# Expert weight loads predicated on the expert of three blocks earlier, in a two-layer graph network with mixtures of experts

## The chip, the cores and the metric

The kernel runs on one core of a Trainium2 chip. The metric is the device time of one execution in microseconds (us), which for one core is the time of that core. A core has TensorE (matrix products, here with a separate record for loading its stationary operand), VectorE, ScalarE, GpSimd and SyncE, each with its own instruction queue that is worked in order, and 16 DMA engines that move data between the device's memory and the on-chip buffer. In the profile they are PE and PEld, DVE, ACT, POOL and SP; "SPq" is SyncE's queue, from which nearly all of this kernel's plain transfers are issued.

## The reference

There are 2708 nodes with 256 features and an adjacency matrix of 2708 x 2708. Two layers follow each other; each has a graph attention and a mixture of experts, both with a residual:

```
x = x + gnn0(layernorm(x), adj)
x = x + moe0(layernorm(x))     # 8 experts, 256 -> 1024 -> 256, gelu, the best 2 of 8 by gate
x = x + gnn1(layernorm(x), adj)
x = x + moe1(layernorm(x))     # 16 experts, 256 -> 512 -> 256, relu, the best 2 of 16
```

The second attention works in hyperbolic coordinates and ends in a sigmoid between exponential and logarithmic maps; the second mixture adds its input and ends in a layer norm with gamma and beta. A mixture computes, for each token, the gate logits, takes the two best experts, and sums their outputs with the softmax of the two logits as weights. All is float32.

## The kernel before

Tokens lie in 22 tiles of up to 128. Each attention multiplies, for a pair of tiles or a tile, the masked weights with all nodes' rows, and accumulates in PSUM. While that runs, the tokens of finished tiles are normalised, gated and routed.

Routing (class `Router`) sorts tokens into pages of 128 rows in device memory, `rows_d`. Tokens are numbered group by group: in layer 0 a group is a pair of tiles, in layer 1 the groups end at tiles 6, 12, 18 and 22. In each group, every expert first fills what is left of its open page and then takes new pages, in the order of the experts. GpSimd scatters each token's row to its two places (L668).

`Experts.plan` gives the pages to blocks: a first stage in page order for pages that are already full (two early stages in layer 1), and the rest when all groups are numbered. It leaves two small tables in the on-chip buffer: `where[0][b]`, the expert of block b, and `where[1][b]`, its first row. Layer 0 works through 47 blocks and layer 1 through 45; a few further blocks (`rest`) stand under a branch that is taken only when more pages are in use.

For a block, `fetch` (L752, L754) brings the 128 rows, `turn` transposes them on TensorE, `hide` (L869) multiplies with the first weights w1, `bend` (L873) applies gelu or relu on ScalarE, `sum_hidden` (L884, L887) multiplies with the second weights w2, `scaled` (L893) weighs on VectorE, and `add` (L898) adds the rows to the sums in device memory by an indirect DMA from GpSimd. Adds of even and odd blocks go to two different sums, and each waits for the last one to the same sums.

The weights of block b go to room b % 3, one of three buffers. `choose` (L734) reads the block's expert from the table into a register of SyncE; `load_w1` (L738) and `load_w2` (L742) issue a DMA each, 1 MB each in layer 0 and 0.5 MB each in layer 1, with the expert as the address's offset. A load of w1 waits until the hidden matmuls of block b - 3 are done, and a load of w2 until its output matmuls are done, since they free the room. Every block loads its weights, whatever is in the room.

The order of each queue is written out while the program is built. In layer 0, `run` sets it by hand: `choose` and w1 of block b + 2, hidden matmuls of b, transposes of b + 1, outputs of b - 1, w2 of b + 2, rows of b + 3. In layer 1, `stream` starts three pieces (`fetcher`, `loader`, `compute`), and a planner (`Clock`) merges them with the routing of the last groups by assumed times. In the steady part of layer 1, SyncE's queue repeats: w2, a row fetch, `choose` of the next block, its w1, its w2. Engines and queues were given a fixed order then (`manual_schedule`), so a wait at the head of SyncE's queue holds all that stands behind it.

After layer 1's blocks the sums are fetched, added on TensorE, normalised, scaled and stored.

Of the kernel before, what the change touches and what calls it, by code (L numbers as in the profile page):

```python
# [13 lines left out]
ET = mybir.EngineType  # L14
# [8 lines left out]
P = 128  # L23
# [123 lines left out]
def kernel(  # L147
# [25 lines left out]
    nc = tc.nc  # L173
# [526 lines left out]
    where = [sm.tile([1, NB_MAX], I32, name=f"where{k}") for k in range(2)]  # L700
# [6 lines left out]
    class Experts:  # L707
# [23 lines left out]
                             w2[:, :n].rearrange("p (c d) -> p c d", d=D))  # L731

        def choose(self, b):
            self.e = nc.values_load(where[0][0:1, b:b + 1], engines=[ET.SP], min_val=0,  # L734
                                    max_val=self.router.E - 1)

        def load_w1(self, b):
            nc.sync.dma_start(self.rooms[b % 3][0], self.w1[bass.ds(self.e, 1)].rearrange(  # L738
                "o (c p) f -> p (o c) f", p=P))

        def load_w2(self, b):
            nc.sync.dma_start(self.rooms[b % 3][1], self.w2[bass.ds(self.e, 1)].rearrange(  # L742
                "o (c p) d -> p (o c) d", p=P))

        def load(self, b):
            self.choose(b)
# [1214 lines left out]
```

## Time and profile before

| | |
|---|---|
| time, median of 3 runs | 1172.25 us (1169.29 to 1180.15) |
| the profiled execution's own time | 1174.49 us |
| its span | 1172.8 us |
| TensorE matmul / weight load busy | 1056.3 us (90%) / 932.1 us (79%) |
| ScalarE / VectorE / GpSimd busy | 586.8 / 528.2 / 404.4 us |
| DMA moved | 261.99 MB, mean 223 GB/s |
| weight loads, layer 0 | 94 of 1024 KB |
| weight loads, layer 1 | 90 of 512 KB |

The page gives each engine's busy time and then cuts the span into 40 slices of 29.3 us, with a digit for the busy share in tenths. A windows answer gives the same for chosen stretches, in us from the start of the span, with the number of instructions in brackets, the granted clock of TensorE, the mean share of the DMA engines in use and their rate. A timeline answer lists instructions in order of time: start, duration, engine, line, operation, output and inputs, and in square brackets the engine's idle time before it with what ended it. A waits answer gives, for an engine and a line, whom it waited for: us in total, times, longest. An answer on one line lists its instructions with the shortest, median and longest duration in ns.

### The profile page before, as it was taken

The page shows a single profiled execution, that of the slowest core. Times are in us where ns is not written, and L with a number is a line of the kernel's source. Part 1 is how long each engine was busy: PE and PEld are TensorE (multiplying, and loading weights), DVE is VectorE, ACT ScalarE, POOL GpSimd, SP SyncE. Part 2 cuts the span into 40 slices and gives each one's busy share as a digit, 9 for nine tenths or more (in the row PEclk, how much of TensorE's full clock was granted, in tenths as well). Part 3 has the DMA queues.
Part 4 walks back from the last instruction along what each step waited for, and adds up shares of the span by engine and source line. Part 5 has one row for each costly group of instructions (what it writes and reads, how often), then busy time and mean ns, then how long its engine had stood idle before and what let it go on. Part 6 is the DMA issues. An engine that isn't in the chain of part 4 may idle for free. (4 is left out here: it accounts for less than half of the span.)

```text
span 1172.8 us, 20834 instructions
## 1 busy us (share of the span) xinstructions
PE 1056.3 (90%) x6753; PEld 932.1 (79%) x6753; DVE 528.2 (45%) x2024; ACT 586.8 (50%) x1637; POOL 404.4 (34%) x467
## 2 busy tenths in 40 slices
PE   5999999988999999999999769998985899999963
PEld 3888888866789999998999634998985788888852
DVE  7778888856531111101111074647677651111136
ACT  3876676644434444444444257536654444444413
POOL 7521121111242222222222250253465375474425
PEclk9999999998999999999999979999897799999987
DMA  9964544410889999999999589401124699999963
GB/s 292 300 226 146 174 146 170 137 77 31 294 268 304 330 321 320 321 287 334 320 323 319 138 274 267 137 1 30 53 82 154 199 266 309 309 311 328 329 194 113
DMA packets 180793, 261.99 MB, mean 223 GB/s; under 512 B 11087, under 2 KB 148982, under 8 KB 177970
## 3 DMA queue, kind: packets, MB, share of 16 engines
q1 hardware_dynamic: 161862, 237.16, 60.9%
q0 software_dynamic: 18816, 23.42, 10.0%
q8 instruction: 57, 0.93, 0.3%
q14 instruction: 58, 0.48, 0.1%
HBM read 205.54 MB, written 54.99 MB: 222 GB/s over the span
## 5 line engine op out<-in xcount | busy, mean ns | idle before, releaser
L893 DVE TENSOR_SCALAR yo<-out_ps,w 128x256 f32<-128x256 f32 x92 | 44.5, 484 | 426.3 <-PE out_ps L887 426.0
L1214 PE MATMUL att_ps<-g_all,z 128*128 128x257 f32 (+3 forms) x968 | 227.6, 388 | 0.0
L1214 PEld LDWEIGHTS att_ps<-g_all,z 128*128 128x128 f32 (+3 forms) x968 | 177.6, 189 | 36.3 <-issue 8.7
L887 PE MATMUL out_ps<-room,ht 128*128 128x256 f32 x872 | 201.6, 383 | 0.0
L887 PEld LDWEIGHTS out_ps<-room,ht 128*128 128x128 f32 x872 | 162.9, 193 | 21.5
L869 PEld LDWEIGHTS hid_ps<-xt,room 128*128 128x128 f32 x1504 | 174.8, 192 | 3.5 <-ACT xt L854 0.8
L869 PE MATMUL hid_ps<-xt,room 128*128 128x128 f32 x1504 | 176.0, 275 | 0.7 <-ACT xt L854 0.5
L1200 ACT ACTIVATE zr<-e_bc,minus_one,g_all 128x256 f32<-128x256 f32 (+3 forms) x242 | 130.7, 591 | 56.8 <-DVE z L1203 56.0
L898 POOL DMA_INDIRECT sums<-yo,xg x43 | 66.9, 1556 | 244.2 <-DVE side L861 131.7
L873 ACT ACTIVATE ht<-hid_ps,w_t 128x128 f32<-128x128 f32 x376 | 128.2, 364 | 23.4 <-PE hid_ps L869 4.1
L668 POOL DMA_INDIRECT rows_d<-xr,place x88 | 92.0, 1046 | 124.7 <-DVE xr L437 77.0
L1565 PE MATMUL att_ps<-half,wide_mask 128*128 128x258 f32 (+1 forms) x968 | 125.9, 292 | 2.4 <-ACT h_all L1502 1.5
L1565 PEld LDWEIGHTS att_ps<-half,wide_mask 128*128 128x128 f32 (+1 forms) x968 | 122.6, 196 | 3.8 <-ACT h_all L1502 2.4
L1203 DVE SCALAR_TENSOR_TENSOR z<-zr,mask_t 128x256 f32<-128x256 f32 (+3 forms) x242 | 98.9, 430 | 32.7 <-ACT zr L1200 17.0
L873 ACT ACTIVATE ht<-hid_ps,w1x 128x128 f32<-128x128 f32 x180 | 65.2, 364 | 96.2 <-PE hid_ps L869 91.6
L898 POOL DMA_INDIRECT sums<-yo,xr x45 | 70.1, 1557 | 82.4 <-DMA sums<-yo,xr 27.8
L863 ACT ACTIVATE w<-xg,side 128x1 f32<-128x1 f32 x43 | 12.7, 295 | 167.6 <-DVE side L861 167.6
L455 PE MATMUL tr_ps<-ident,xr 128*128 128x128 f32 (+1 forms) x222 | 41.1, 296 | 35.0 <-DVE xr L437 15.9
L1425 POOL CAST wide_mask<-mask_t 128x1408 fp32r<-128x1408 fp8e4 x31 | 42.5, 1377 | 84.6 <-PE att_ps L1565 84.6
L869 PE MATMUL hid_ps<-lo,wide_mask 128*128 128x128 f32 x480 | 64.4, 289 | 5.7 <-DMA wide_mask<-in_L_ffn_w_dram 5.5
L869 PEld LDWEIGHTS hid_ps<-lo,wide_mask 128*128 128x128 f32 x480 | 60.5, 202 | 11.2 <-issue 10.5
L455 PEld LDWEIGHTS tr_ps<-ident,xr 128*128 128x128 f32 (+1 forms) x222 | 29.7, 155 | 42.9 <-issue 18.7
(287 smaller groups left out, 1435.6 us busy)
## 6 DMA issues: line engine op xcount, KB each, us to landing
room<-in_L_ffn_W_dram SPq DMA_DIRECT2D x94, 1024.0 KB
wide_mask<-in_L_ffn_w_dram SPq DMA_DIRECT2D x60, 512.0 KB
room<-in_adj_dram SPq DMA_DIRECT2D x20, 1354.0 KB
room<-in_L_ffn_w_dram SPq DMA_DIRECT2D x30, 512.0 KB
rows_d<-nobody SPq DMA_DIRECT2D x1, 7511.0 KB
rows_d<-nobody SPq DMA_DIRECT2D x5, 1295.0 KB
sums<-nobody SPq DMA_DIRECT2D x2, 2944.0 KB
xr<-rows_d SPq DMA_DIRECT2D x45, 129.5 KB
```

Of the source, the lines that this page charges most:

```text
L455: nc.tensor.transpose(ps[:, c, :r], src[:, c * P:(c + 1) * P], ident[:r, :r])
L668: ins = nc.gpsimd.indirect_dma_start(out=self.rows_d[:, :], in_=self.rows[t][:r], in_offset=None, out_offset=bass.IndirectOffsetOnAxis(ap= ...
L869: nc.tensor.matmul(ps[:, :P], w1_b[:, c, f * P:(f + 1) * P], xt[:, c, :], start=(c == 0), stop=(c == DC - 1))
L873: nc.scalar.activation(ht[:, f, :], ps[:, :P], self.func, bias=self.bias[:, f, b:b + 1])
L887: nc.tensor.matmul(ps[:, :D], ht[:, f, :], self.rooms[b % 3][1][:, f, :], start=False, stop=(f == self.FC - 1))
L893: nc.vector.tensor_scalar(yo, ps[:, :D], w, None, op0=OP.mult)
L898: ins = nc.gpsimd.indirect_dma_start(out=self.sums[k][:, :], in_=yo, in_offset=None, out_offset=bass.IndirectOffsetOnAxis(ap=self.rows.pop ...
L1200: nc.scalar.activation(zr[:k, :n], e_bc[:k, lo:lo + n], AF.Relu, bias=minus_one[:k], scale=g_all[:k, j, D + 1:D + 2])
L1203: nc.vector.scalar_tensor_tensor(z[:k, :n], zr[:k, :n], 1.0, mask_t[:k, j // 2, lo:lo + n, j % 2], op0=OP.add, op1=OP.mult)
L1214: nc.tensor.matmul(accs[i][:r, :D + 1], z[:k, q * P:q * P + r], g_all[:k, j, :D + 1], start=(j == 0), stop=(j == LAST))
L1425: nc.gpsimd.tensor_copy(m, src)
L1565: nc.tensor.matmul(accs[i][:, :D + 2], wide_masks[i, j % 2][:k, j // 2, :], half_k[:k, j, :], start=(j == 0 and half_k is halves[0]), stop ...
```

## The change

From block 3 on, `choose` reads a second table entry, the expert of block b - 3, which is the last block that used the same room. Both weight loads of the block get the condition that the two experts differ. Under a false condition the load is to be left out: the address is made to lie outside the weights, and the transfer is to be dropped while its completion is still counted, so that those who wait for it go on. The first three blocks of a layer load as before. No order in any queue is changed and nothing is given to another engine. In the built program, SyncE has per block from 3 on a second register load with its range check, and before each of the two weight loads two register operations more and a fused register operation with four steps where there were two.

```
         def choose(self, b):
-            self.e = nc.values_load(where[0][0:1, b:b + 1], engines=[ET.SP], min_val=0,
-                                    max_val=self.router.E - 1)
+
+            def expert(b):
+                return nc.values_load(where[0][0:1, b:b + 1], engines=[ET.SP], min_val=0,
+                                      max_val=self.router.E - 1)
+
+            self.e = expert(b)
+            self.when = {"cond": self.e != expert(b - 3)} if b >= 3 else {}
 
         def load_w1(self, b):
             nc.sync.dma_start(self.rooms[b % 3][0], self.w1[bass.ds(self.e, 1)].rearrange(
-                "o (c p) f -> p (o c) f", p=P))
+                "o (c p) f -> p (o c) f", p=P), **self.when)
 
         def load_w2(self, b):
             nc.sync.dma_start(self.rooms[b % 3][1], self.w2[bass.ds(self.e, 1)].rearrange(
-                "o (c p) d -> p (o c) d", p=P))
+                "o (c p) d -> p (o c) d", p=P), **self.when)
```

## The prediction

> **What bounds the kernel now.** I read the page's slices first, to find the stages, then the windows, to see what is full in each.
>
> ```profile
> PE   5999999988999999999999769998985899999963
> DMA  9964544410889999999999589401124699999963
> GB/s 292 300 226 146 174 146 170 137 77 31 294 268 304 330 321 320 321 287 334 320 323 319 138 274 267 137 1 30 53 82 154 199 266 309 309 311 328 329 194 113
> ```
>
> A slice is 29.3 us. The experts of layer 0 run in slices 11 to 22 (about 300 to 665 us), those of layer 1 in slices 31 to 38 (908 to 1121 us). Both fill TensorE and the DMA engines at once, so the slices alone don't say which one is last.
>
> ```profile
> core 0: us, PE busy (x) PEld busy (x) DVE busy (x) ACT busy (x) POOL busy (x), PEclk, DMA share, GB/s
> 440.00:520.00 80.00, 80.00 (x556) 75.28 (x555) 7.74 (x31) 34.59 (x110) 17.03 (x11) 1.00 0.99 317
> 968.00:1116.00 148.00, 139.20 (x947) 124.79 (x946) 23.28 (x105) 63.56 (x209) 75.05 (x63) 1.00 1.05 315
> ```
>
> In layer 0 TensorE has no gap. The first relu or gelu of each block in the timeline (L873, ACT) gives a block's period: 7.36 us for nearly every layer-0 block, with a jitter of 0.01. That is TensorE's own pace; a weight load ends no wait there. In layer 1 it is different:
>
> ```profile
> 968.03 1.65 ACT L873 ACTIVATE ht<-hid_ps,w1x 128x128 f32<-128x128 f32 x4 [0.22 <-PE hid_ps L869]
> 1116.13 0.37 ACT L873 ACTIVATE ht<-hid_ps,w1x 128x128 f32<-128x128 f32 x1 [2.33 <-PE hid_ps L869]
> ```
>
> These are blocks 9 and 44: 148.10 us for 35 blocks, 4.23 each. Of the 35 periods 14 are 3.84 and none is shorter, so 3.84 is TensorE's floor, and 148.10 - 35 x 3.84 = 13.7 us is stall. What ends it, for the hidden matmuls of 968 to 1120 us:
>
> ```profile
>   issue: 16.4, 21
>   DMA wide_mask<-in_L_ffn_w_dram: 5.5, 10
>   DMA room<-in_L_ffn_w_dram: 3.1, 4
> ```
>
> The named part is the first weight half (w1) landing late; "issue" is mostly the weight-load side of the same gaps. So 13.7 us is the most that lighter weight traffic can give in this stretch. Before block 9 the gaps have other owners (routing on VectorE, the rows' scatter), and TensorE's clock is 0.59 to 0.77 from 900 to 940 us.
>
> The queue that issues the loads is the other thing to read. SyncE in two blocks of that stretch:
>
> ```profile
> 1041.64 0.37 SPq L742 DMA_DIRECT2D wide_mask<-in_L_ffn_w_dram  x1
> 1042.84 0.35 SPq L754 DMA_DIRECT2D xr<-rows_d  x1
> 1043.95 0.37 SPq L738 DMA_DIRECT2D wide_mask<-in_L_ffn_w_dram  x1
> 1045.49 0.38 SPq L742 DMA_DIRECT2D wide_mask<-in_L_ffn_w_dram  x1
> ```
>
> and its waits from 960 to 1120 us:
>
> ```profile
> SPq L742 <- PE out_ps L887: 43.0, 34, 3.6
> ```
>
> One block is w2 (L742), a row fetch (L754), the choice of the next expert, w1 (L738), and again w2, which waits for the outputs of three blocks ago. From 1041.64 the queue stands at the next w2 at about 1044.55: 2.91 us of work (the median; the mean over the stretch is 3.04), then it waits. At the floor of 3.84 only 0.93 us per block is free. That is the number the change has to be measured against.
>
> **What the Trainium skill says.** "DMA: Bandwidth & Descriptors", section "Issuing engines are not separate DMA queues": all issuers share the same 16 DMA engines and interleave. The trace agrees (share 1.05 with SyncE's loads and GpSimd's adds together), so a load left out frees time for the rest. Its section "Latency and other measured facts" gives a register load from memory ("`tensor_load` floor") about 600 ns; this trace has 272 ns, and I use that. No page read here prices a DMA that is predicated off.
>
> **The change, part by part.** *What is removed.* Routing decides it. I counted picks per expert from the reference's gate logits and laid out pages as the kernel does. Layer 0 spreads over all 8 experts: of its 44 blocks from block 3 on, one (34) has the expert of three blocks earlier. Layer 1 collapses: 2708, 2697 and 11 picks go to experts 9, 11 and 15, and 20 of 42 blocks qualify (3-5, 9-11, 15-17, 21, 22, 24, 28-30, 34-36, 40, 44), 17 of them after block 8. A block carries 1.05 MB of weights, 0.13 MB of rows and some 0.26 MB for the add's read and write; 20 skips leave out 21 MB of layer 1's 47 MB. Blocks that skip don't wait for bytes; blocks that don't, mostly after skipped ones, find an emptier queue. A w1 issued at 1040.13 now lets its block start at 1045.43, 5.3 us later; packets of such a load take about 84 ns, 16 per engine, so alone I estimate 3.4 us. A w1 issued 2.3 after the w2 before it (1037.80) is needed 7.6 after that w2, so traffic would no longer stall TensorE. Taken alone: up to -13.7 us.
>
> *What is added, all of it on SyncE's queue.* Rows for the price:
>
> ```profile
> L734 SPq TENSOR_LOAD <-where x92: 263/272/963, 292.1 to 1107.1; - x92
> L734 SPq FUSED_REGOPS  x92: 152/152/159, 292.5 to 1107.5; - x92
> L734 SPq SEQ_ASSERT  x92: 18/18/18, 292.7 to 1107.7; - x92
> L742 SPq FUSED_REGOPS  x92: 37/37/42, 293.4 to 1108.6; - x92
> ```
>
> One more register load per block: 0.27 + 0.15 + 0.02, with three gaps of 0.05 between instructions, 0.59 us. Before each of the two loads, two register operations (multiply, compare) are new, and the fused operation has four steps for two. The trace shows no single register operation; between 0.03 (the MOVE beside it) and 0.15 (the fused check), I take 0.04, with a gap of 0.05: 0.18 a load. The longer fused one adds between 0.03 and 0.15, I take 0.10. Two loads: 0.56 (0.40 to 0.80). Together 1.15 us a block, between 1.0 and 1.4. A predicated-off DMA still stands in the queue; issued, it costs 0.37. [...] 0.1 is a lower end; refusing an address may go a slow way, so I allow 0.9. I take 0.27.
>
> *The sum.* SyncE per block: 3.04 + 1.15 - (17 of 36 blocks x 2 x 0.10 = 0.09) = 4.10, less about 0.05 since slowed issues (register loads above 0.4, a DMA issue of 0.85) come from a full queue: 4.05. This is over the floor of 3.84, so the free 0.93 us is gone and SyncE sets the pace: what is late next is the issue of w1, not its bytes. 35 x (4.23 - 4.05) = -6.3 us. At entry SyncE is already behind: the row fetch waits for the scatter until 953.2, and w2 of block 8 goes out at 957.28 without a wait. Blocks 7 and 8 cost it 2.3 us more, and block 8 starts right on its w1 now: some +1.5. Against it, w1 has about that much slack before TensorE notices a lag: -1.5. The row fetch queued behind is wanted about 6 us after its issue, so a lag of 1 to 2 us is covered; GpSimd's adds follow TensorE. The last landing and the norm move up whole.
>
> *Layer 0.* SyncE stands about 4.5 us of each 7.36 at w2, so 1.15 us is hidden; without that cover it would cost 44 x 1.15. A w1 issued at 485.63 landed at 494.06 and is used at 497.60, slack 3.5 us for a shift of 0.9. One exception: the fetch of the next layer's weights holds the queue from 513.9 to 522.9 and block 28 then stalls 3.9; that grows by +0.9.
>
> Total -6.3 + 1.5 - 1.5 + 0.9 = -5.4 us. The profiled execution took 1174.49 (span 1172.8, 1.7 around it), 2.24 over the median of 1172.25. 1174.49 - 5.4 = 1169.1; less 2.24 is **1166.9, about 1167**.
>
> **The rivals.**
> *SyncE keeps up* (25 in 100). If the added work stays below 0.93 us, by cheap register operations or quick skips, TensorE runs at 3.84 throughout: -13.7 + 0.9 gives 1159.5. For it: SyncE's mean wait of 1.2 us per block; against it: the register load alone takes 0.59 of it.
> *SyncE becomes the bound at a worse pace than the DMA is now* (15 in 100), the case on the other side. The place is w1's issue; the price is each predicated-off DMA. It decides from a SyncE loop of 4.23 us: 3.04 + 1.15 - 0.05 = 4.14 with skips as dear as issues, so a skip of 0.47 us for 0.37 (0.94 skips a block) already ends the gain. At 0.9 the loop is 4.64: 35 x 0.41 + 0.9 = +15, 1187; at 0.65 it is 4.40: +7, 1179. Against it: the neighbouring sequencer instructions are all under 0.4.
> *The loads aren't left out* (7 in 100), since the kernel's routing differs or the refused DMA still moves bytes: w1 is issued 0.9 later into an unchanged queue, adding a part of it to the 21 gaps, about +5, 1177.
> *Forecast* (53 in 100): SyncE-bound at 3.95 to 4.15, 1162 to 1172.
>
> **How the numbers follow.** Predicted is the forecast's 1167. The range reaches down to the first rival's 1159 and up to 1179, over the cheaper half of the slow case. A difference under 1% (11.7 us) is about what this kernel's measurement can't tell from no change: the runs shown span 1169 to 1180. Most of the first rival passes 1160.5 (0.20), as do a few forecasts with an early region that gains too (0.03): 0.23 faster. The dear half of the second case passes 1184: 0.09. The rest, 0.68, is within 1%.
>
> **What would show it.** Right: DMA bytes fall by about 22 MB; layer 0's period stays 7.36; layer 1's GB/s falls to about 200 to 240; SyncE's wait at w2 nearly goes; periods lie near 4.05, with gaps before hidden matmuls also where the load was skipped. Wrong: the wait at w2 stays and the periods are 3.84 (first rival); predicated-off issues longer than 0.5 us (second); unchanged bytes (third); or layer 0 loses its steady period, for which I see no cause.

## The result, and the profile after

The changed kernel takes 1169.33 us (median of 20 runs, 1166.2 to 1177.73) where the kernel before, run beside it, takes 1175.28 (1169.29 to 1180.15). The ratio is 0.9967, with a 95% interval of 0.9952 to 0.9983, so it is 0.33% faster, about 3.9 us. (The two medians lie 5.95 us apart; the ratio uses all twenty runs of each, and from here on it is the measure.) A second group of runs on another chip gave 0.9959 (0.9944 to 0.9974). The profiled execution took 1168.86 us, its span is 1167.1.

The slices of the page after, in the same order as before (TensorE, DMA engines, GB/s, then the total of the DMA packets):

```profile
PE   5999999987999999999999859998985898999963
DMA  9964445410889999999899589500224487777963
GB/s 297 297 213 161 168 149 176 135 78 27 295 276 283 314 326 323 320 291 344 260 314 321 158 270 243 176 1 7 76 82 135 121 207 193 188 206 203 251 193 111
DMA packets 163486, 238.96 MB, mean 205 GB/s; under 512 B 10415, under 2 KB 137046, under 8 KB 160658
```

In slices 34 to 38, layer 1 moves 188 to 251 GB/s in place of 309 to 329, and its DMA engines are 70 to 90% busy. The total of the packets falls from 261.99 to 238.96 MB, by 23.0. (The page's line "HBM read 205.54 MB" is the same for both kernels. A kernel further down, in which the loads are left out at build time, has 182.47 there and 238.91 MB in packets. So that line seems to count what the program asks for; the packets show what was moved.) Layer 0 looks as before. The windows of the two stretches:

```profile
core 0: us, PE busy (x) PEld busy (x) DVE busy (x) ACT busy (x) POOL busy (x), PEclk, DMA share, GB/s
440.00:520.00 80.00, 80.00 (x558) 75.38 (x558) 8.34 (x33) 34.84 (x110) 17.12 (x11) 1.00 1.00 322
968.00:1116.00 148.00, 139.31 (x957) 127.62 (x955) 24.32 (x108) 64.75 (x210) 76.78 (x64) 1.00 0.79 202
```

A third of the traffic is gone from the second window, yet the first relus of blocks 9 and 44 in the timeline are still 144.56 us apart (148.10 before):

```profile
965.67 0.76 ACT L878 ACTIVATE ht<-hid_ps,w1x 128x128 f32<-128x128 f32 x2 [0.22 <-PE hid_ps L874]
1110.23 0.37 ACT L878 ACTIVATE ht<-hid_ps,w1x 128x128 f32<-128x128 f32 x1 [1.92 <-PE hid_ps L874]
```

At the floor of 3.84 a block it would be 134.4. The lines now stand five lower (L874 for the hidden matmul, L743 for w1, L747 for w2). Who ends the waits of 960 to 1120 us, first at the hidden matmul, then at w2 in SyncE's queue:

```profile
PEld hid_ps L874 <- issue: 11.5, 11, 2.2
...
PE hid_ps L874 <- DMA wide_mask<-in_L_ffn_w_dram: 5.5, 6, 1.8
...
PE hid_ps L874 <- DMA room<-in_L_ffn_w_dram: 2.3, 3, 1.0
```

```profile
SPq L747 <- PE out_ps L892: 15.3, 19, 2.1
```

The named waits for w1 add up to 7.8 us; before they were 8.6. With a third fewer bytes, TensorE waits for w1 nearly as long as before. And SyncE, which waited 43.0 us at w2 before, still waits 15.3: it is not the bound on average.

The prices, from the lines of the choice (L736) and of w1 (L743); durations are min/median/max in ns:

```profile
L736 SPq TENSOR_LOAD <-where x178: 261/268/1796, 293.0 to 1101.7; - x178
L736 SPq FUSED_REGOPS  x178: 147/147/165, 293.3 to 1102.0; - x178
L743 SPq ALU_OP  x172: 37/38/52, 315.8 to 1102.4; - x172
L743 SPq FUSED_REGOPS  x92: 42/56/56, 293.6 to 1102.5; - x92
L743 SPq DMA_DIRECT2D wide_mask<-in_L_ffn_w_dram x30: 73/372/413, 889.8 to 1099.9; - x30
```

A load that is predicated off is the 73 ns of the last row (the shortest of the 30), against 372 for one that is issued. Two skipped issues in the timeline (block 16), and then the pair of blocks that shows what goes wrong (18 and 19, which both load):

```profile
990.88 0.07 SPq L743 DMA_DIRECT2D wide_mask<-in_L_ffn_w_dram  x1
991.93 0.07 SPq L747 DMA_DIRECT2D wide_mask<-in_L_ffn_w_dram  x1
...
999.12 0.40 SPq L743 DMA_DIRECT2D wide_mask<-in_L_ffn_w_dram  x1
999.94 0.38 SPq L747 DMA_DIRECT2D wide_mask<-in_L_ffn_w_dram  x1
...
1003.05 0.37 SPq L743 DMA_DIRECT2D wide_mask<-in_L_ffn_w_dram  x1
1003.84 0.37 SPq L747 DMA_DIRECT2D wide_mask<-in_L_ffn_w_dram  x1
```

```profile
1003.97 0.37 ACT L878 ACTIVATE ht<-hid_ps,w1x 128x128 f32<-128x128 f32 x1 [1.92 <-PE hid_ps L874]
...
1009.26 0.37 ACT L878 ACTIVATE ht<-hid_ps,w1x 128x128 f32<-128x128 f32 x1 [3.37 <-PE hid_ps L874]
```

Block 18's w1 goes out at 999.12 into an empty queue and lands at 1002.14, when the last of its packets ends, after 3.0 us. Block 19's w1 goes out at 1003.05, 3.11 after block 18's w2, and lands at 1007.99, after 4.9. From landing to first relu takes 1.3 us, so the relu is at 1009.26: 5.29 after block 18's, 1.45 over the floor. The same two blocks before:

```profile
1002.05 0.37 SPq L742 DMA_DIRECT2D wide_mask<-in_L_ffn_w_dram  x1
...
1004.46 0.37 SPq L738 DMA_DIRECT2D wide_mask<-in_L_ffn_w_dram  x1
```

```profile
1006.98 0.37 ACT L873 ACTIVATE ht<-hid_ps,w1x 128x128 f32<-128x128 f32 x1 [1.92 <-PE hid_ps L869]
...
1010.82 0.37 ACT L873 ACTIVATE ht<-hid_ps,w1x 128x128 f32<-128x128 f32 x1 [1.92 <-PE hid_ps L869]
```

There block 19's w1 was issued 2.41 after block 18's w2 and 2.52 ahead of block 18's relu, and landed at 1009.31, also after 4.9 us; TensorE didn't notice. After the change it is issued only 0.92 ahead of that relu. I call this distance, from a block's w1 issue to the first relu of the block before it, the **lead** of w1.

Over the whole stretch the same split shows. From here on I count blocks 12 to 44 (33 periods, floor 126.8 us), from the first relus of the timeline, and part the stalls (what a period is over 3.84) into the 14 blocks whose loads can be left out and the 19 that must load. Lead and landing are means over the 19:

| profile | stall, 14 that can skip | stall, 19 that load | mean lead of w1 | mean w1 issue to landing |
|---|---|---|---|---|
| before | 5.2 | 8.1 | 2.70 | 5.35 |
| after | 0.0 | 10.1 | 1.71 | 4.52 |

The skipped blocks give all they can. The loading blocks' landing becomes 0.83 us shorter and the lead 0.99 shorter, so they stall more than before.

### The profile page after: what moved, and what is told of

Same layout as the page of the kernel before. It is cut to its first block, busy times and chain, and to the rows that moved or that the text cites. A ratio compares the mean times of both kernels' runs of the same rounds, so it can differ in the third digit from the quotient of the medians.

```text
span 1167.1 us, 21436 instructions
## 1 busy us (share of the span) xinstructions
PE 1051.8 (90%) x6753; PEld 932.8 (80%) x6753; DVE 527.4 (45%) x2024; ACT 586.5 (50%) x1637; POOL 404.6 (35%) x467
## 2 busy tenths in 40 slices
DMA packets 163486, 238.96 MB, mean 205 GB/s; under 512 B 10415, under 2 KB 137046, under 8 KB 160658
## 3 DMA queue, kind: packets, MB, share of 16 engines
HBM read 205.54 MB, written 54.99 MB: 223 GB/s over the span
## 5 line engine op out<-in xcount | busy, mean ns | idle before, releaser
L874 PEld LDWEIGHTS hid_ps<-xt,room 128*128 128x128 f32 x1504 | 174.9, 192 | 3.0 <-ACT xt L859 0.8
L874 PE MATMUL hid_ps<-xt,room 128*128 128x128 f32 x1504 | 175.9, 275 | 0.5 <-ACT xt L859 0.5
L874 PE MATMUL hid_ps<-lo,wide_mask 128*128 128x128 f32 x480 | 63.9, 288 | 5.5 <-DMA wide_mask<-in_L_ffn_w_dram 5.5
L874 PEld LDWEIGHTS hid_ps<-lo,wide_mask 128*128 128x128 f32 x480 | 61.1, 202 | 8.8 <-issue 7.8
```

What stands on the lines that cost most here:

```text
L874: nc.tensor.matmul(ps[:, :P], w1_b[:, c, f * P:(f + 1) * P], xt[:, c, :], start=(c == 0), stop=(c == DC - 1))
```

## The experiments

Theory 1: the changed kernel's stalls are w1's lateness, from what was added ahead of it on SyncE. Theory 2: they are bytes, in runs of loading blocks. Theory 3, the prediction's: SyncE's mean pace. The chips of these groups differ: the kernel before takes 1199.13 us on the first group's chip and 1175.1 to 1175.4 on the others. Blocks 0 to 11 of layer 1, part of which run at half clock, took 79.3 us on the first chip and 68.2 and 67.1 on two others with one and the same kernel (the kept register, below). So whole times are given as ratios to the kernel before on the same chip, and stalls for the stretch above. There the clock was full, but for 3.4 us at half in four of the eighteen profiles, which makes 1.7 us of the stall counted in each: the changed kernel's second, never false, early choice in the kernel before, and the kernel before without adds. A single profile's stall scatters: see the repeated ones.

**The kernel before again, and the changed one again.** No edit.

> The kernel before, unchanged, profiled on the chip of this group of runs, since chips differ in how long their TensorE clock is held down. From block 11 to block 44 of layer 1 (33 periods, floor 126.8 us) it took 140.0 in the first profile, 13.2 us of stall. Theory 1 (w1's lead time) and theory 2 (bytes) both expect 12 to 15 us of stall again; the stretch is at full clock, so it should carry over from chip to chip even where the whole span doesn't.

> The changed kernel, unchanged, for the same reason. Block 11 to 44: 136.9 us in its first profile, 10.1 us of stall; expected again within 1.5 us. Time against the kernel before: 0.995 to 0.998. What comes before layer 1 should be the same in both kernels within the scatter of single executions.

> The changed kernel once more, as the base on the chip of this group: its two profiles so far have 10.1 and 10.3 us of stall between block 11 and block 44 of layer 1. If the chip of the first group was the kinder one (there the kept register left 3.9 us, and on another chip kept register and early choice together left 7.9), this shows which of the two it is on.

Before again: 11.5 us of stall (4.1 in the blocks that can skip, 7.4 in those that load; lead 2.69, landing 5.29). After: 10.4 and 13.5 in the two repeats, all of it in loading blocks, leads 1.78 and 1.83, landings 4.52 and 4.91; the ratio 0.9959. So the split of the table holds, and the stalls scatter by 2 to 3 us from profile to profile, more than I expected.

**Never false.** The cost without the benefit.

```diff
-            self.when = {"cond": self.e != expert(b - 3)} if b >= 3 else {}
+            self.when = {"cond": self.e != expert(b - 3) + 64} if b >= 3 else {}
```

> The same register loads, compares and predicates as in the changed kernel, with a comparison that is never false, so that every weight load is done: the cost without the benefit. Theory 1: each loading block issues w1 about 0.8 us later than the kernel before, into the same full queue; the fourteen or so stalls of before grow by part of it, and SyncE's loop of about 3.9 leaves no slack: 5 to 15 us slower than before. Theory 2, bytes: the DMA engines still pace layer 1 at 4.23 a block and the later issue is hidden in the queue: within 2 us of before. Theory 3, SyncE's pace: loop 3.04 + 0.92 = 3.96, under 4.23, hidden: within 2 us of before.

The ratio is 1.0068 (1.004 to 1.0096), 8 us slower. The stall is 19.3 us (12.1 in the blocks that load in the changed kernel, 7.2 in the others), the lead 2.10. SyncE's own work is here about 4.0 us a block (154.4 us for 35 blocks, less 15 of waits), over the floor of 3.84. But the mean period is 4.41, longer than this pace and longer than the 4.23 of before, so neither SyncE's mean pace nor the bytes give it. Theory 1 holds, theories 2 and 3 fail: even into a full queue, a later issue of w1 is paid for.

**Left out at build time.** The benefit without the cost (w2 is edited alike).

```diff
+SAME = ({34}, {3, 4, 5, 9, 10, 11, 15, 16, 17, 21, 22, 24, 28, 29, 30, 34, 35, 36, 40, 44})
...
         def load_w1(self, b):
+            if b in SAME[self.layer]:
+                return
             nc.sync.dma_start(self.rooms[b % 3][0], self.w1[bass.ds(self.e, 1)].rearrange(
```

> The kernel before, with the loads that this routing makes needless left out when the program is built (layer 0 block 34 and the 20 known blocks of layer 1): no added instruction on SyncE, valid for these inputs alone. The benefit without the cost. Theory 1: w1 is issued 0.76 us earlier than in the changed kernel, the stalls of 10.2 us fall to 4 or less: stretch 134.4 to 139, span near 1160. Theory 2, bytes: same bytes as the changed kernel, so same stalls: stretch 144, within 1 us of the changed kernel. Theory 3: the floor, 134.4.

> The loads left out when the program is built, again beside the changed kernel: no added work on SyncE. Theory 1: 3 to 5 us of stall. Theory 2: what bounds it in a run of loading blocks is 1.44 MB per block at about 320 GB/s, 4.5 us against the floor of 3.84; five runs of two or three such blocks, less what the lead of the first one covers, give 7 to 9 us of stall, on a chip that enters the stretch without a pause.

The ratios are 0.9929 (0.9897 to 0.9961) and 0.9933 (0.9907 to 0.996): about 8 us. The stalls are 3.9 and 6.1 us, the leads 3.47 and 3.64; the second stall lies between the two theories' forecasts. So the leaving out alone is worth twice what the change brought, and even it doesn't reach the floor.

**Kept register.** The expert of block b-3 is remembered in its register; the second register load goes, the compares and predicates stay.

```diff
-            self.last_add, self.adds = {}, []
+            self.last_add, self.adds, self.experts = {}, [], {}
...
-            self.e = expert(b)
-            self.when = {"cond": self.e != expert(b - 3)} if b >= 3 else {}
+            old = self.experts.pop(b - 3, None)
+            self.e = self.experts[b] = expert(b)
+            self.when = {} if old is None else {"cond": self.e != old}
```

> The changed kernel, with the expert of block b-3 kept in its register, so that the second register load of each block (0.58 us on SyncE) is gone and the two compares and the predicates stay. Theory 1, w1's lead time: the nine stalls of the changed kernel's layer 1 (10.2 us between block 9 and block 44) are w1 landing late because it is issued late; 0.58 us earlier takes about 0.5 us from each, 4 to 5 us in all: span near 1162.5, stretch near 140. Theory 2, bytes: w1 lands when the w2 ahead of it has drained, and being issued earlier moves nothing: stretch stays 144.6, within 1 us of the changed kernel. Theory 3, SyncE's mean pace (the prediction's): the mean loop falls from 3.68 to about 3.1, but it was below the floor of 3.84 already: no change either.

> The kept register again, to be set beside the changed kernel on one chip. Theory 1, w1's lead time: stall at least 4 us below the changed kernel's of this group, about 4 to 6 us, wherever it runs. Theory 2, bytes: the 3.9 us of the first group was the chip's doing (there TensorE's throttle held blocks 8 to 10 back by some 6 us, which let SyncE and the transfers catch up), and on a chip without that it stays at 8 to 10 us.

> The kept register with all adds, as the base of this group: 4 to 8 us of stall, and 0.990 to 0.994 of the kernel before. Against the changed kernel's 0.9967 and 0.9959, this also fixes whether the second register load costs as much as 4 us of the whole, about half of what the skipped loads bring.

The ratios are 0.993, 0.9913 and 0.9936 (intervals 0.9903 to 0.9957, 0.9885 to 0.994, 0.9911 to 0.9961), 7.5 to 10 us faster than before. Stalls are 4.0, 7.9 and 7.2 us, leads 2.01 to 2.22. The second register load thus cost about half of what the skipped loads can bring, and the compares and predicates together cost nothing that shows beside the loads left out at build time. This version is faster than the kernel before and, as far as the runs tell, than the changed one: against the changed kernel's 0.9952 to 0.9983 and 0.9944 to 0.9974, the second group's interval doesn't touch either, and the other two overlap them in part. (No chip timed both kernels over many runs.) Theory 1 is right about the fall on the second group's chip, from 13.5 to 7.9 us of stall, but it left only 4 to 6 us; 7.9 is nearly theory 2's 8 to 10. So lateness is a part of the stall and not all of it. (The 6 us that the second forecast lays to the throttle are the stall of block 9 in the first profile; the clock was at half for 3.4 us there, which explains 1.7 of them.)

The same pair of blocks in the second group, block 18's w2 and block 19's w1 on SyncE, and then their first relus:

```profile
998.57 0.38 SPq L748 DMA_DIRECT2D wide_mask<-in_L_ffn_w_dram  x1
...
1001.11 0.37 SPq L744 DMA_DIRECT2D wide_mask<-in_L_ffn_w_dram  x1
```

```profile
1002.92 0.37 ACT L879 ACTIVATE ht<-hid_ps,w1x 128x128 f32<-128x128 f32 x1 [1.92 <-PE hid_ps L875]
...
1007.04 0.37 ACT L879 ACTIVATE ht<-hid_ps,w1x 128x128 f32<-128x128 f32 x1 [2.19 <-PE hid_ps L875]
```

w1 follows w2 after 2.54 us, the lead is 1.81, and of the 1.45 us of stall 0.28 is left.

**Early choice.** The registers for block b+1 are loaded ahead of block b's w2, where SyncE would stand at its wait.

```diff
+                chosen = {}
...
-                    self.choose(b)
+                    if b not in chosen:
+                        self.choose(b)
+                        chosen[b] = self.e, getattr(self, "when", None)
+                    self.e, self.when = chosen[b]
                     self.load_w1(b)
                     clock.moved(Mark(), 1.7, 2.0)
+                    if 3 <= b < NB - 1 and stage(b + 1) == stage(b):
+                        self.choose(b + 1)
+                        chosen[b + 1] = self.e, getattr(self, "when", None)
+                        self.e, self.when = chosen[b]
                     if b >= 3:
                         yield out_at[b - 3]
+                    self.e, self.when = chosen[b]
                     self.load_w2(b)
```

> The changed kernel, with the choice of block b+1's expert (both register loads) moved ahead of block b's w2 on SyncE, where the queue would stand waiting for the outputs of block b-3; nothing is left out, and SyncE's work per block is the same. Theory 1: w1 follows w2 after about 1.9 us instead of 3.0, so stalls of up to about 1.1 us vanish: 10.2 falls to 2 or 3, stretch 137, span near 1160. Theory 2, bytes: as the changed kernel, stretch 144. Theory 3, SyncE's mean pace: the loop's work is the same, so as the changed kernel.

> The early choice again. Theory 1: 5 to 6 us of stall. Theory 2: 8 to 10. The time against the kernel before was 0.995 in the first group, no better than the changed kernel's 0.996 and 0.997 elsewhere; about that again.

The ratios are 0.9947 (0.9931 to 0.9963) and 0.9948 (0.9932 to 0.9964), the stalls 5.6 and 10.0 us. The gain over the changed kernel is too small to tell, and the means fall short of the kept register's on the same two chips (0.993 and 0.9913), though the intervals overlap. The stalls fit neither theory twice: the first forecast of theory 1 was 2 to 3, and 10.0 is theory 2's. The lead grew to 2.32 and 2.72, as meant, but landing grew too, to 5.34 us in the second group. The waits at w2 (first the early choice, then the kept register, second group both):

```profile
SPq L747 <- PE out_ps L892: 14.6, 15, 2.6
```

```profile
SPq L748 <- PE out_ps L893: 36.5, 35, 2.5
```

With the early choice SyncE waits at w2 as little as in the changed kernel (15.3). In runs of loads its w2 goes out 0.47 us ahead of the first relu of the block before, against 0.51 to 0.57 in the three profiles of the changed kernel: no earlier, and the earlier w1 stands behind it. Why this does worse than the kept register, whose w1 follows w2 later (after 2.5 us in place of 1.9), is not shown. Work moved within SyncE's queue gave little here; work taken off it gave more.

**Early choice alone, in the kernel before; and both remedies together.** The edits are the two above.

> The kernel before, with no predicate, and the choice of block b+1's expert moved ahead of block b's w2. All loads are done. Theory 1, w1's lead time alone: w1 is issued some 0.5 us earlier after w2, and the stalls, up to twenty of 0.1 to 2.6 us, lose up to 0.5 each: 13.2 falls to 7 or 8, about -6 us. Theory 2, bytes: every block moves 1.05 MB of weights and the rows in 3.84 to 4.23 us, the DMA engines set the pace, and an earlier issue into a full queue lands no earlier: stall stays 11 to 14, time within 2 us of before. I expect theory 2 to hold for this kernel, where nothing is left out, and theory 1 for the changed one.

> The changed kernel with both remedies: the expert of block b-3 kept in its register, and the choice of block b+1 moved ahead of block b's w2. w1 then follows w2 after some 1.9 us with a loop of about 3.1 us. Theory 1: lead time was all that was wrong, so 1 to 3 us of stall are left of 10.1 (3.9 with the kept register alone, 5.5 with the early choice alone): time 0.990 to 0.993 of before. Theory 2, bytes: what the kept register leaves (3.9 us, in the second and third block of a run of loads) is landing behind the w2 ahead, which no earlier issue shortens: 3 to 4 us are left, as with the kept register alone.

The first is 1.000 (0.9985 to 1.0015), with 11.3 us of stall, a lead of 3.25 and a landing of 5.96: w1 had 0.55 us more lead and took 0.6 us longer to land, as theory 2 has it for a full queue (the kernel before had 11.5 and 13.2 us of stall). Both together are 0.9926 (0.9902 to 0.9949) with 8.0 us of stall, no better than the kept register alone and more than either theory left: the lead rises to 2.70, the landing to 5.34. So there is a point from which an earlier issue buys nothing here. Whether what is left is transfer, the next runs try.

**Without the adds.** Three kernels leave out the adds of layer 1's blocks 12 to 43, so part of layer 1's result is missing; SyncE's instructions and the weight queue are untouched.

```diff
         def add(self, b, yo):
             k = b % 2
+            if self.layer and 12 <= b < 44:
+                del self.rows[b]
+                return
```

> The kernel before, leaving out the adds of layer 1's blocks 12 to 43 into the sums (GpSimd's transfers, so that part of layer 1's result is not computed): per block some 1.18 MB in place of 1.44. Theory 2, bytes: before, the DMA engines pace layer 1; with 1.18 MB at 320 GB/s, 3.7 us a block, under the floor of 3.84: stall between blocks 11 and 44 falls from 11.4 to 13.3 us to 4 or less. Theory 1, w1's lead: w1 is issued 2.4 us after the w2 ahead of it as before, so the stall stays above 9.

> The changed kernel, leaving out the same adds. Theory 2: its 10 to 13 us of stall are bytes in runs of loading blocks and fall to 4 or less. Theory 1: they are w1 issued 3.1 us after the w2 ahead of it and 1.8 us before the previous block's first relu; landing takes some 4 us even with the engines otherwise free, against 1.8 + 3.84 - 1.3 = 4.3 that the lead allows, so 3 to 7 us stay. Mixed, which I expect: about 4.

> The changed kernel with the expert of block b-3 kept in its register, leaving out the same adds. Theory 2: what the kept register leaves (4 to 8 us) is bytes, so 2 us or less stay. Theory 1: the same 4 to 8.

The ratios are 0.9915 (before), 0.9898 (changed) and 0.9882 (kept register), from 4 to 6 runs each. The windows of 1020 to 1105 us, in the order before, after, before without adds, after without adds:

```profile
1020.00:1105.00 85.00, 80.47 (x550) 72.26 (x549) 13.30 (x60) 37.21 (x124) 46.56 (x43) 1.00 1.05 321
```

```profile
1020.00:1105.00 85.00, 82.03 (x569) 75.44 (x567) 13.97 (x63) 38.24 (x126) 46.66 (x43) 1.00 0.85 224
```

```profile
1020.00:1105.00 85.00, 84.60 (x585) 79.19 (x585) 13.98 (x63) 39.56 (x130) 14.17 (x22) 0.98 0.92 300
```

```profile
1020.00:1105.00 85.00, 85.00 (x600) 79.87 (x599) 14.73 (x68) 40.41 (x135) 14.16 (x22) 1.00 0.62 195
```

In the last one TensorE has no gap left in 85 us, although w1 is on the mean issued no earlier than in the changed kernel (lead 1.47): it now lands 3.80 us after its issue, under the 1.47 + 3.84 - 1.3 = 4.0 that the lead allows. From block 21 to 44 its stall is 0.1 us, against 4.9, 3.8 and 7.8 in the three profiles of the changed kernel. In blocks 19 to 43 the first packet of a w1 comes 1.0 to 2.4 us after its issue with the adds and 1.0 to 1.2 without them. The loads that stand alone gain nothing: block 18's w1 lands after 3.0 us in both kernels, block 19's, behind a w2, after 4.9 with the adds and 3.9 without.

So lateness alone isn't enough and bytes alone aren't either: in this stretch a w1 of the changed kernel stalls TensorE where its lead is short **and** the adds share the DMA engines while it lands. That it is their share of the engines, and not something else that leaving them out frees, is argued from these landings.

The totals over all 33 periods say less. They are 9.7 us (before), 5.5 (changed) and 4.8 (kept register), and all three lie where theory 1 put them. What stays is mostly at the start: blocks 12 and 13, whose loads come when adds of blocks up to 11, which are not left out, can still be under way, stall 2.8 us (changed) and 3.2 us (kept register), and the changed kernel has one stall of 2.29 at block 20. The kept register keeps another 1.6 us from block 21 on, 1.2 of it at block 43. I hadn't expected the kernel before to keep 9.7 us of its 11.5 to 13.2. Of these 8.0 are at blocks 12, 13, 22 and 23, with the 1.7 of half clock at block 23; from block 24 on it stalls 0.8 us, where its two profiles with adds have 4.8 and 4.1. So there too most of the steady stalls went with the adds. Each of these stalls is from one profile.

## Why the prediction was right or wrong

The number was near: 1167 forecast, 1169.33 measured, in the range and in the forecast's own 1162 to 1172; -5.4 us forecast against -3.9 and -4.8. That it came near was luck, since the reason given for it was wrong: the stretch from block 9 to 44 was to give -6.3 us because SyncE would set a pace of 4.05; it gave -3.5 in the first pair of profiles and -1.4 in the mean of all five, and SyncE does not set the pace there. A statement about measuring was too modest as well: that 1% is about what can't be told from no change. Twenty runs of each resolve 0.33% with an interval of 0.15% on either side, so a small gain was to be forecast as a gain, where I put most of the chance on no change.

1. *What bounds the kernel, and the count of skips*: right. Stalls before hidden matmuls of late w1s; 20 of 42 blocks of layer 1 skip, 23.0 MB for "about 22" (its own terms, 20 x 1.05 and 2.1 for layer 0's block 34, add up to 23).
2. *The register load*, 0.59 us: right, +0.58 (268 + 147 + 18 ns and the gaps).
3. *The register operations and the skip*: mis-sized, all on the dear side. Per load the two operations and the longer fused one were to cost 0.28 and cost 0.17 (2 x 38 ns, two gaps of 35, +19). A predicated-off DMA was taken at 0.27 and took 0.073. The whole is 0.92 us for a loading block, not 1.15, and the forecast's sum for SyncE's mean loop, taken again with these, is 3.68, not 4.05. Whether slowed issues come from a full queue, for which 0.05 was taken off, stays open: from 965 us on, two register loads were over 0.4 us before and three after, and two weight issues over 0.45 before and none after.
4. *"SyncE sets the pace: what is late next is the issue of w1, not its bytes"*: this step failed. With its own right sizes (3.68 under the floor of 3.84) it would have led to the first rival, TensorE at 3.84 throughout and 1159.5, which is as wrong. In place of a slower pace for all blocks the profile shows 24 of 33 periods at the floor and nine loading blocks that hold nearly all of the 10.1 us of stall, since w1's mean lead fell from 2.70 to 1.71 us. SyncE waits 15.3 us at w2 and still issues w1 too late: its waiting is done at w2, and all that was added ahead of w1 comes after that wait. A mean over a loop can't show that; the distance from w1's issue to its use can. The sharper view would have been a table of lead and landing by block, from the same timeline that I read for two instants.
5. *"So traffic would no longer stall TensorE"*: failed as well. The estimate of 3.4 us for a landing alone was fair (3.0 to 3.4 in blocks 18, 25 and 31, each the first after skipped ones), though the working shown, 16 packets of 84 ns, gives 1.3 of it. But the forecast took one load alone. In the second and third block of a run of loads landing takes 4.3 to 6.6 us (block 26 alone 3.0), and the mean over the 19 is 4.5 to 4.9. The -13.7 that was to be had at most was never within reach: with no added work at all, 3.9 to 6.1 us stay.
6. *Entry, +1.5 and -1.5*: no loss shows. From block 0 to 11 it took 67.5 and 67.4 us before, 66.6, 66.1 and 67.1 after.
7. *Layer 0, +0.9 at block 28*: not seen. The period was 11.24 us in the first profile before, 10.31 in the second, and 10.31 in the first after; in the steady part the other periods are 7.36 as forecast.
8. *What would show it*: GB/s of about 200 was right. Wrong were periods near 4.05, gaps where the load was skipped (none), and a wait at w2 that nearly goes (a third is left).

The third rival (nothing left out) and the second (a skip of 0.47 us or more) are ruled out by the 23.0 MB and the 73 ns.

The saved time isn't located in full. In the mean of two profiles before and three after, the 33 periods give 1.0 us, the entry 0.8, the rest nothing clear; 4 were measured over many runs. Single profiled executions scatter too much to place the remainder. How the stalls at blocks 12 and 13 come about was not tried.

## What to carry to other kernels

A load left out helps the blocks that skip it; what is added to decide it is paid by the blocks that don't, at the instruction queued right behind. Read both: list for each block how long before its use a load is issued and how long it takes to land, and look for added instructions between a wait and the next urgent issue. Moving them ahead of the wait gave little here; taking one off, by remembering a value in a register in place of reading it again, about doubled the gain.

## What was not expected of the hardware

- A DMA predicated off holds SyncE's queue for 73 ns, an issued one for 372; a register operation takes 38 ns and a gap of 35. The register load is 268 ns here; the Trainium skill, "DMA: Bandwidth & Descriptors", section "Latency and other measured facts", gives about 600 as a floor, which this trace contradicts; the page doesn't say where its load reads from, and here it is a table in the on-chip buffer.
- An emptier queue doesn't make a load free. The same section gives some 600 ns to the first byte of such a DMA; block 18's w1 (issued 999.12, issue done 999.52) has its first packet at 1000.16, 0.64 later, which agrees if the time is counted from the end of the issue. A deep queue hides this: in the kernel before, for all 33 blocks an earlier load's packet is still under way when w1's first one starts, while in the changed kernel the load queue stands idle for 0.4 to 1.5 us before the first packet in 6 of the 19 loading blocks.
- The adds weigh more in engine time than in bytes. By queue, in 1020 to 1105 us of the changed kernel (packets, MB, share of the 16 engines; q0 are GpSimd's adds, q1 SyncE's loads):

```profile
q1 hardware_dynamic: 13195, 16.20, 60.2%
q0 software_dynamic: 3016, 2.75, 24.1%
```

Of the two queues together, q0 is 15% of the bytes and 29% of the time. A 1 KB packet of the adds takes 119 ns on the mean, a 1 KB packet of w2 49. The prediction counted a read and a write for each add, which is twice the bytes and covers most of this. The skill's section "Queues, rings and completion order" of the same page says that each DMA engine takes turns between the queues that have work; that fits a w1 which lands earlier once the adds are gone, though no run here shows the turns themselves.
- A stall of TensorE can cost more than itself. In the four profiles with half clock inside the stretch, the clock fell about when TensorE resumed after a stall of 2.3 to 3.8 us, for 3.4 us, which lost another 1.7. In the kernel before without adds this is the whole 1.65 us at block 23, whose w1 had landed in time. Stalls of 2.9 (block 12 of the same profile) and 2.6 us (block 23 of the first one before) went by without it, so what decides is not shown.
- In the changed kernel without adds, the one late stall (block 20, 2.29 us, w1 landing 6.1 us after its issue) has a transfer of the instruction stream under way meanwhile, one 16 KB packet of 1.6 us (by queue, over 1009 to 1015 us: packets, MB, share of the 16 engines). That it is the cause is argued from the coincidence only.

```profile
q8 instruction: 1, 0.02, 1.7%
```
